# An S4-gated feed-forward kernel: two roots of the layer norm through ScalarE, one LoRA product in four row groups, and a reordered start

## The chip, the cores and the metric

The kernel runs on one core of a Trainium2 chip. The time is the device time of one launch in microseconds (us), the median of repeated runs. A profiled execution also has a span, from its first to its last recorded instruction; the rest of its time lies around the span.

The engines are named as in the profile: PE is TensorE's matmul (PEld its weight load), DVE is VectorE, ACT is ScalarE, POOL is GpSimd, SP is SyncE, which here only issues DMA transfers.

## The reference

The input `x` has 2 x 1024 tokens of 512 features, all in float32. What is computed, cut to what matters:

```python
xn = layernorm(x)                       # over the 512 features, eps 1e-5
s  = causal_convolution(xn) + D * xn    # along each row of 512, kernel from an S4 state space (64 states)
h1 = xn @ w1.T + 2 * (xn @ A1.T) @ B1.T # hidden width 1376, LoRA rank 16
h3 = xn @ w3.T + 2 * (xn @ A3.T) @ B3.T
g  = silu(h1) * h3
ffn = g @ w2.T + 2 * (g @ A2.T) @ B2.T  # back to 512
out = x + s * silu(ffn)
```

The convolution is written in the reference with FFTs over rows of 512 values.

## The kernel before, in words

The tokens are handled as four blocks of 512 (`x_in[0]` to `x_in[3]`), each of four tiles of 128 tokens by 512 features. Two blocks make a super-block. The first half of the kernel makes `g` from the blocks and stores it in DRAM (`g_dram`); the second half multiplies by `w2`, makes the convolution, the gate and the output.

The matrix products are cut in Strassen-like fashion: sums and differences of quarters of an operand are formed on DVE, and seven products (numbered 1 to 7, called steps) take the place of eight. In the first half this is done at two levels. The hidden width is split into five pairs of 256 columns (`w_pair[0]` to `w_pair[4]`) and a last part of 96 columns (`w_last`). A `Chain` is one set of seven steps. It accumulates in three PSUM banks with the tags `x`, `w` and `y` (each tag has two banks, `bank(tag)` hands them out in turn; a fourth tag is `aux`). ACT copies snapshots out of `x` and `w`, DVE adds in `y` (L779) and the kept sums (L869), ACT applies Silu (L828), POOL multiplies (L836) and adds (L869).

LoRA is folded into the weights: `lora_product` (L382) multiplies the two factors of rank 16 into a PSUM bank, and `merge` (L392) adds twice that to the weights in SBUF. The factors stand in SBUF at partitions 0, 32, 64 and 96 (the groups 0 to 3; groups 0 and 2 hold the factors of `w1`, 1 and 3 those of `w3`). `merge_pair` uses groups 0 and 1 alone and makes one half of a pair (four products); it is used for the first pair, twice. `merge_whole_pair` uses all four groups in turn (eight products), for all later pairs.

The norm: `norm_stats` (L247, L248) takes mean and variance on DVE; `norm_root` (L281 to L284) makes the reciprocal root and the shift, with eight operations of `rsqrt` (L57 to L66) on DVE; `normalize` works on ACT (tiles 0 and 2, L293) and POOL (tiles 1 and 3, L297). `norm_root` is called for block 0, for block 1, and once for blocks 2 and 3 together. Block 3's sums and squares are taken on ACT (`act_sums` L254, `act_squares` L265) with small steps on POOL. `transpose` turns the tiles on PE (L304) and copies them on ACT: into `xr` for blocks 0 and 2 (L312), into `b12` and `xr` for blocks 1 and 3 (L314, L315).

The order on each engine is the program's own (a manual schedule). In the first half it comes from a list of events with places: `at(place, what)` puts a step on a heap, which is emptied in the order of the places, and `after(delay, what)` puts one behind the current place. The places are written by hand. The steps around the change are:

- before the heap: `keep_warm` (L990, products of the identity with itself, 18 before the LoRA of the last part and 4 after it), `lora_last`, the norm of block 0 and its transposes, the statistics of block 1, `merge_last`;
- on the heap: `normalize(1)`, the last part's sums on POOL (`last_sums`), the first pair's LoRA, the transposes of block 1 into the `y` banks, the sums of token operands (`outer_token_sum`, L328) and of weights (`outer_weight_sums`, L440; `inner_weight_sum`, L452), the statistics of block 2, the sums of block 3, and so on. `inner_token_sum` (L340 to L346) makes the second level of token sums into `t_in`; the statement in `norm_root` writes `veps` (L281).

The DMA requests go out on SP (some of the first on ACT) in the order in which the program names them. Requests take turns on eight semaphores, so that a request waits until the one eight places before it has landed. The first lines of that order are:

```python
x_in = {0: load_x(0)}
...
for v, f in enumerate(factors):
    load_lora((nc.sync, nc.scalar)[v], v, *f, LSPLIT, HID)
nc.scalar.activation(warm, warm, AF.Silu)
x_in[1] = load_x(1)
w_last, s_last = load_last()
w_pair, s_pair = {0: load_pair(0)}, {c: {} for c in range(NPAIR)}
x_in[2], x_in[3] = load_x(2), load_x(3)
w_pair[1] = load_pair(1)
for v, f in enumerate(factors):
    load_lora(nc.sync, 2 + v, *f, LSPLIT, HID)
```

The activation of `warm` (L972) brings the activation table of Silu in at the start.

Of the kernel before, what the change touches and what calls it, by code (L numbers as in the profile page):

```python
# [12 lines left out]
F32 = mybir.dt.float32  # L13
# [4 lines left out]
P = 128  # L18
# [3 lines left out]
HID = 1376  # L22
# [27 lines left out]
def rsqrt(nc, pool, v, shape):  # L50


    y = pool.tile(shape, F32, tag="rs_y", name="rs_y")
    t = pool.tile(shape, F32, tag="rs_t", name="rs_t")
    part = 3.0 / 8.0
    c2 = part * 0.703952253
    nc.vector.tensor_scalar(  # L57
        y.bitcast(I32), v.bitcast(I32), -0.5, float(0x5F1FFFF9), ALU.mult, ALU.add
    )
    nc.vector.tensor_tensor(t, y, y, ALU.mult)  # L60
    nc.vector.scalar_tensor_tensor(t, t, -c2, v, ALU.mult, ALU.mult)
# [46 lines left out]
def s4_gated_ffn(  # L108
# [110 lines left out]
    def after(delay, what):  # L219
        at(now[0] + delay, what)  # L220
# [4 lines left out]
    def load_x(b):  # L225
        room = (None, None, t_in[4], t_in[6])[b]
        tiles = []
        for tt in range(NTT):
            t = value() if room is None else room[:, tt, :]
            queue = nc.scalar if b == 0 and tt % 2 else nc.sync  # L230
            queue.dma_start(out=t, in_=x[bass.ds(b * TB + tt * P, P), :])
            tiles.append(t)
        return tiles
# [41 lines left out]
            norms[b][:, :, 1], sums_of_x[b][:, 2, :], 1.0 / DIM, None, mult  # L275
        )

    def norm_root(mv, *blocks):
        n = len(blocks) * NTT
        veps = small.tile([P, n], F32, tag="veps", name="veps")  # L280
        nc.vector.tensor_scalar(veps, mv[:, :, 1], EPS, None, add)  # L281
        rstd = rsqrt(nc, small, veps, [P, n])
        shift = small.tile([P, n], F32, tag="shift", name="shift")
        nc.vector.scalar_tensor_tensor(shift, mv[:, :, 0], -1.0, rstd, mult, mult)  # L284
        for n, b in enumerate(blocks):
            norms[b] = [t[:, n * NTT : (n + 1) * NTT] for t in (rstd, shift)]
# [12 lines left out]
    def transpose(b, tiles, tag="aux"):  # L299
        sb, low = divmod(b, 2)  # L300
        for tt in tiles:
            ps = bank(tag)
            for dc in range(NDC):
                nc.tensor.transpose(  # L304
                    ps[:, dc * P : (dc + 1) * P],
                    x_in[b][tt][:, dc * P : (dc + 1) * P],
                    ident,
                )
            at_ = slice(tt * P, (tt + 1) * P)
            halves = ps.rearrange("p (c k t) -> p c k t", c=2, k=2)  # L310
            if low == 0:
                nc.scalar.copy(xr[:, 0:2, sb, :, at_], halves)  # L312
            else:
                nc.scalar.copy(b12[sb][:, :, at_], halves[:, 0])  # L314
                nc.scalar.copy(xr[:, 2, sb, :, at_], halves[:, 1])  # L315
# [64 lines left out]
    def lora_product(ps, group, dc, lo, n, start=True):  # L380
        d, h = lora_factors(group, lo, n)
        nc.tensor.matmul(  # L382
            ps,
            lhsT=d[:, dc * P : (dc + 1) * P],
            rhs=h,
            start=start,
            stop=True,
            skip_group_check=True,
        )

    def merge(to, ps):
        nc.vector.scalar_tensor_tensor(to, ps, LORA_SCALE, to, mult, add)  # L392
# [11 lines left out]
                )  # L404
        return w

    def merge_pair(c, w, half, tag="aux"):

        ps = [bank(tag), bank(tag)]
        for k in range(2):  # L410
            for v in range(2):
                n = slice(k * 2 * P, (k + 1) * 2 * P)
                lora_product(ps[v][:, n], v, 2 * half + k, PAIR_AT[c], 2 * P, k == 0)
        for v in range(2):
            to = w[:, (1, 2, 0, 3)[2 * v + half]].rearrange("p k m h -> p (k m h)")
            after(1.6 + v, lambda to=to, v=v: merge(to, ps[v]))
# [45 lines left out]
    def load_last():  # L462
        both = const.tile([P, 2, 2 * NDC * LASTR], F32, tag="w2b", name="last")
        w, s = (
            both[:, i].rearrange("p (a b h) -> p a b h", a=n, h=LASTR)
            for i, n in enumerate((2, 4))
        )
        for v, src in enumerate((w1T, w3T)):
            nc.sync.dma_start(
                out=w[:, v], in_=src[:, LAST * P :].rearrange("(dc p) h -> p dc h", p=P)  # L470
            )
        return w, s

    def lora_last():
        ps = [bank("y"), bank("y")]
# [487 lines left out]

    x_in = {0: load_x(0)}
    warm = const.tile([P, 1], F32, name="warm")
    nc.gpsimd.memset(warm, 0.0)
# [5 lines left out]
    nc.scalar.activation(warm, warm, AF.Silu)  # L972
    x_in[1] = load_x(1)
    make_upper_triangular(nc, tri, 1.0, diag=True)
    w_last, s_last = load_last()
    w_pair, s_pair = {0: load_pair(0)}, {c: {} for c in range(NPAIR)}
    x_in[2], x_in[3] = load_x(2), load_x(3)
    w_pair[1] = load_pair(1)
    for v, f in enumerate(factors):
        load_lora(nc.sync, 2 + v, *f, LSPLIT, HID)  # L980

    def other_factors():
        for v, (_, h) in enumerate(factors):
# [18 lines left out]
    ps_last = lora_last()  # L1002
    mv = norm_tile(0)
    norm_stats(0, range(NTT))
    norm_root(mv, 0)
    normalize(0)

    keep_warm(primed[1], 4)
    transpose(0, range(NTT))
    mv = norm_tile(1)  # L1010
    norm_stats(1, range(2))
    merge_last(w_last, ps_last, 0)
    norm_stats(1, range(2, NTT))
    norm_root(mv, 1)
    merge_last(w_last, ps_last, 1)
    mv_late = norm_tile(2, 3)
    ab_last = last_operands(w_last, s_last)

# [573 lines left out]
```

## Time and profile before

| what | value |
|---|---|
| time, median of 3 runs | 442.49 us (442.27 to 443.13) |
| profiled execution: time / span | 442.57 us / 440.8 us |
| PE busy | 433.5 us, 98% of the span |
| DVE busy | 316.9 us, 72% |
| POOL busy | 209.3 us, 47% |
| ACT busy | 144.2 us, 33% |
| granted PE clock | 0.998 of full speed |
| DMA moved | 53.61 MB, mean 122 GB/s over the span |
| chain that ended last | PE 84%, DVE 10%, issue 2%, ACT 2%, DMA 1% |

The page gives shares over the whole span. The start can be read only from the timelines: they list each engine's instructions in order of time, with start, length, engine, line, operation, output, input, and in brackets the idle time before it and what ended that. A count such as x8 may name records: an ordinary float32 product leaves two records, a transpose one. The chain of waits follows the last instruction back, at each step to what released it or to the instruction before it on its engine.

In the first 20 us the transfers run at 218 to 379 GB/s and the DMA engines are full from 5 us on; PE has its first product at 1.37 us (the priming ones) and its first transposes at 10.45.

### The profile page before, as it was taken

The numbers are of one execution on the slowest core, as the hardware profiler recorded it, in microseconds if no ns is written. First come the engines' busy times: TensorE is split into PE (matmuls) and PEld (weight loads), VectorE is DVE, ScalarE is ACT, GpSimd is POOL, SyncE is SP. The second block draws the span as 40 slices with busy tenths as digits, with TensorE's granted clock in tenths as the row PEclk, the third lists the DMA queues.
The fourth block names the chain that finished last, engine by engine and source line by source line (L and its number), as shares of the span: only waits on it lengthen the run. The fifth ranks groups of instructions, "written<-read, shape, count | busy, mean of one in ns | idle before, by whom it ended". The sixth has DMA issues, their size and how long they took to land.

```text
span 440.8 us, 5156 instructions
## 1 busy us (share of the span) xinstructions
PE 433.5 (98%) x1704; PEld 268.5 (61%) x1704; DVE 316.9 (72%) x534; ACT 144.2 (33%) x296; POOL 209.3 (47%) x156
## 2 busy tenths in 40 slices
PE   7999999999999999999999999999999999999996
PEld 7545333444444444444443447888898999999995
DVE  5899999946974597469746796979786875753234
ACT  2777242453245324532453242211101212112221
POOL 2325469995689368936894469400000123222221
PEclk9999999999999999999999999999999999999999
DMA  8921304025002400350045526395902833423211
GB/s 258 370 66 47 116 0 149 24 72 168 25 24 96 143 24 25 99 160 24 25 148 187 167 90 214 112 348 200 342 22 75 306 115 95 144 97 95 88 57 48
DMA packets 35466, 53.61 MB, mean 122 GB/s; under 512 B 4688, under 2 KB 21520, under 8 KB 35312
## 3 DMA queue, kind: packets, MB, share of 16 engines
q1 hardware_dynamic: 35088, 52.69, 36.9%
q10 hardware_dynamic: 352, 0.60, 0.4%
q8 instruction: 13, 0.21, 0.2%
q14 instruction: 13, 0.11, 0.1%
HBM read 33.88 MB, written 19.40 MB: 121 GB/s over the span
## 4 chain that ended last, share of the span: by engine, by line
PE 84%; DVE 10%; issue 2%; ACT 2%; DMA 1%; POOL 0%; SPq 0%; DVEq 0%; POOLq 0%
PE x L755 42%; PE y L755 21%; PE w L755 11%; PE aux L929 4%; PE w L929 2%; DVE s L452 1%; DVE t_in L342 1%; DVE xt L328 1%; DMA s<-in_x_dram 1%; DVE t_in L340 1%; DVE w L440 1%; DVE s L779 1%; PE y L382 1%; PE y L528 1%; PE aux L710 1%
## 5 line engine op out<-in xcount | busy, mean ns | idle before, releaser
L1310 POOL TENSOR_TENSOR o<-o,xin 128x512 f32<-128x512 f32 (+1 forms) x17 | 23.3, 1369 | 132.9 <-DVE o L1309 132.9
L836 POOL TENSOR_TENSOR s<-c,s 128x512 f32<-128x512 f32 (+1 forms) x44 | 63.1, 1439 | 16.1 <-ACT c L828 10.9
L775 ACT COPY s<-x 128x512 f32<-128x512 f32 (+1 forms) x54 | 31.6, 584 | 86.8 <-PE x L755 86.7
L755 PE MATMUL x<-t_in,s 128*128 128x512 f32 (+1 forms) x148 | 55.4, 501 | 0.0
L779 DVE TENSOR_TENSOR s<-s,y 128x512 f32<-128x512 f32 (+1 forms) x54 | 36.0, 679 | 17.2 <-PE y L755 12.1
L869 POOL TENSOR_TENSOR s<-ua_three,s 128x512 f32<-128x512 f32 x20 | 35.9, 1793 | 25.7 <-DVE s L779 25.7
L755 PEld LDWEIGHTS x<-t_in,s 128*128 128x128 f32 x148 | 26.6, 190 | 23.3 <-issue 12.0
L869 POOL TENSOR_TENSOR ua_three<-ua_three,s 128x512 f32<-128x512 f32 x20 | 33.0, 1652 | 15.1 <-DVE s L779 15.1
L755 PE MATMUL y<-t_in,s 128*128 128x256 f32 (+1 forms) x108 | 35.8, 458 | 0.0
L1332 ACT COPY z<-x 128x256 f32<-128x256 f32 x24 | 8.8, 371 | 70.5 <-PE x L755 70.4
L1307 DVE TENSOR_TENSOR aux<-aux,m 128x384 f32<-128x384 f32 x32 | 18.1, 565 | 15.8 <-PE aux L929 14.3
L869 POOL TENSOR_TENSOR s<-u_three,s 128x512 f32<-128x512 f32 x20 | 28.5, 1430 | 1.8 <-ACT c L828 1.0
L828 ACT ACTIVATE c<-c 128x512 f32<-128x512 f32 x40 | 25.2, 632 | 10.0 <-DVE c L869 10.0
L755 PEld LDWEIGHTS y<-t_in,s 128*128 128x128 f32 x108 | 20.2, 190 | 11.1 <-issue 9.3
L793 ACT COPY w<-x 128x512 f32<-128x512 f32 (+1 forms) x37 | 21.1, 570 | 12.2 <-PE x L755 12.2
L869 POOL TENSOR_TENSOR u_three<-ua_three,u_three 128x512 f32<-128x512 f32 x10 | 15.6, 1557 | 11.6 <-DVE u_three L779 11.5
L755 PE MATMUL x<-t_in,w 128*128 128x512 f32 x40 | 20.9, 603 | 0.0
L755 PE MATMUL x<-xr,s 128*128 128x512 f32 x40 | 20.6, 616 | 0.2 <-DVE ua_one L869 0.2
L755 PE MATMUL x<-xt,w 128*128 128x512 f32 x40 | 20.7, 598 | 0.0
L755 PE MATMUL x<-xr,w 128*128 128x512 f32 x40 | 20.6, 614 | 0.0
L755 PE MATMUL x<-xt,s 128*128 128x512 f32 x40 | 20.4, 592 | 0.0
L440 DVE TENSOR_TENSOR w<-w 128x512 f32<-128x512 f32 x20 | 20.1, 1015 | 0.1
(302 smaller groups left out, 906.0 us busy)
## 6 DMA issues: line engine op xcount, KB each, us to landing
g_dram<-s SPq DMA_DIRECT2D x40, 256.0 KB, 2.1
g<-g_dram SPq DMA_DIRECT2D x10, 512.0 KB, 5.6
xin<-in_x_dram SPq DMA_DIRECT2D x16, 256.0 KB, 2.8
out_dram<-o SPq DMA_DIRECT2D x14, 256.0 KB, 2.0
t_in<-g_dram SPq DMA_DIRECT2D x6, 512.0 KB, 4.2
w<-in_w1T_dram SPq DMA_DIRECT2D x10, 256.0 KB, 3.3
w<-in_w3T_dram SPq DMA_DIRECT2D x10, 256.0 KB, 5.0
t_in<-in_x_dram SPq DMA_DIRECT2D x8, 256.0 KB, 5.5
```

Source lines behind the costliest of these rows:

```text
L440: nc.vector.tensor_tensor(*sums[name])
L755: nc.tensor.matmul(ps[:, cols], lhsT=lhsT, rhs=rhs if parts == 1 else rhs[:, cols], start=first and i == 0 and part == 0, stop=i == len(pa ...
L775: nc.scalar.copy(t, self.x)
L779: nc.vector.tensor_tensor(t, t, self.y, add)
L793: nc.scalar.copy(self.w, self.x)
L828: nc.scalar.activation(c, c if src is None else src, AF.Silu)
L836: nc.gpsimd.tensor_tensor(g, act, g, mult)
L869: (nc.vector if o < 20 else nc.gpsimd).tensor_tensor(to, a, b, add)
L929: nc.tensor.matmul(to[:, n * P : (n + 1) * P], lhsT=x_, rhs=by, start=start, stop=True, skip_group_check=True,)
L1307: nc.vector.tensor_tensor(y[:, P:], y[:, P:], m[:, n * P : (n + 3) * P], add)
L1310: (nc.vector if last else nc.gpsimd).tensor_tensor(o, o, self.xin[h][:, cols], add)
L1332: nc.scalar.copy(t, xb)
```

## The change

The change has four parts, and moves some places with them.

- `norm_root` gets a flag `on_act`, set for blocks 0 and 1. Then `refined` takes the root on ACT (`AF.Sqrt`, with `eps` as its bias), the reciprocal on DVE, and one Newton step on DVE (three operations). `norm_root` of blocks 2 and 3 keeps `rsqrt`. The first activation of `warm` is now a Sqrt, and a second one, of Silu, follows the root of block 1. There is one priming product more (5).
- The first pair's LoRA is made by `merge_whole_pair` in one lot, into the two `y` banks and the two `aux` banks, ahead of block 1's transposes. `merge_pair` goes. The first tile of block 1 is transposed into a borrowed `x` bank, the other three into the `y` banks.
- The factors of groups 2 and 3, needed for that, are requested before the first pair's weights rather than after the second pair's.
- The request for `w1` of the last part stands ahead of block 1's tiles; that for `w3` stays behind them.
- Places: three of block 2's four statistics move behind the first pair's sums (0.84 to 0.9, before -5.2 to -3.6); the merge of the last part's `w3` comes ahead of the second root; `normalize(2)` and `normalize(3)` move from 7.3 and 7.7 to 7.7 and 7.75. With that ACT copies block 1's four tiles before the last part's first Silu, and a snapshot of `ua_three` before it normalizes block 2.

```diff
+    def refined(mv, veps):
+        shape = list(veps.shape)
+        y = small.tile(shape, F32, tag="rs_y", name="rs_y")
+        t = small.tile(shape, F32, tag="rs_t", name="rs_t")
+        root = small.tile(shape, F32, tag="root", name="root", bufs=1)
+        nc.scalar.activation(root, mv[:, :, 1], AF.Sqrt, bias=eps)
+        nc.vector.tensor_scalar(veps, mv[:, :, 1], EPS, None, add)
+        nc.vector.reciprocal(y, root)
+        nc.vector.tensor_tensor(t, y, y, mult)
+        nc.vector.scalar_tensor_tensor(t, t, -0.5, veps, mult, mult)
+        nc.vector.scalar_tensor_tensor(y, t, 1.5, y, add, mult)
+        return y
...
-        rstd = rsqrt(nc, small, veps, [P, n])
+        if on_act:
+            rstd = refined(mv, veps)
+        else:
+            nc.vector.tensor_scalar(veps, mv[:, :, 1], EPS, None, add)
+            rstd = rsqrt(nc, small, veps, [P, n])
...
-    nc.scalar.activation(warm, warm, AF.Silu)
+    nc.scalar.activation(warm, warm, AF.Sqrt)
+    w_last, s_last, load_of_last = load_last()
+    load_of_last(0)
     x_in[1] = load_x(1)
+    load_of_last(1)
     make_upper_triangular(nc, tri, 1.0, diag=True)
-    w_last, s_last = load_last()
+    for v, f in enumerate(factors):
+        load_lora(nc.sync, 2 + v, *f, LSPLIT, HID)
     w_pair, s_pair = {0: load_pair(0)}, {c: {} for c in range(NPAIR)}
     x_in[2], x_in[3] = load_x(2), load_x(3)
     w_pair[1] = load_pair(1)
-    for v, f in enumerate(factors):
-        load_lora(nc.sync, 2 + v, *f, LSPLIT, HID)
...
-    norm_root(mv, 0)
+    norm_root(mv, 0, on_act=True)
     normalize(0)
-    keep_warm(primed[1], 4)
+    keep_warm(primed[1], 5)
...
     norm_stats(1, range(2, NTT))
-    norm_root(mv, 1)
     merge_last(w_last, ps_last, 1)
+    norm_root(mv, 1, on_act=True)
+    nc.scalar.activation(warm, warm, AF.Silu)
...
-    at(-9, lambda: merge_pair(0, w_pair[0], 0))
-    at(-3.8, lambda: merge_pair(0, w_pair[0], 1))
-    for i in range(2):
-        at(-6 + i, lambda i=i: transpose(1, range(2 * i, 2 * i + 2), "y"))
+    at(-9, lambda: merge_whole_pair(
+        0, w_pair[0], [bank("y"), bank("y")], (1.6, 1.7, 1.8, 1.9)))
+    at(-6, lambda: transpose(1, (0,), "x", True))
+    at(-5.9, lambda: transpose(1, range(1, NTT), "y"))
...
-        at(-6 + 0.8 * tt, lambda tt=tt: norm_stats(2, (tt,)))
+        at((-6, 0.84, 0.85, 0.9)[tt], lambda tt=tt: norm_stats(2, (tt,)))
...
-    at(7.3, lambda: normalize(2))
-    at(7.7, lambda: normalize(3, (0,)))
+    at(7.7, lambda: normalize(2))
+    at(7.75, lambda: normalize(3, (0,)))
```

More of the change, by code (lines that the diff above doesn't have):

```diff
@@ L276, in act_variances, with norm_root @@
         )
-    def norm_root(mv, *blocks):
+    def refined(mv, veps):
[10 more added lines that the diff above has]
+        return y
+    def norm_root(mv, *blocks, on_act=False):
         n = len(blocks) * NTT
         veps = small.tile([P, n], F32, tag="veps", name="veps")
-        nc.vector.tensor_scalar(veps, mv[:, :, 1], EPS, None, add)
-        rstd = rsqrt(nc, small, veps, [P, n])
+        if on_act:
[3 more added lines that the diff above has]
+            rstd = rsqrt(nc, small, veps, [P, n])
         shift = small.tile([P, n], F32, tag="shift", name="shift")
@@ L297, in normalize, with transpose @@
                 nc.gpsimd.tensor_scalar(t, t, rstd[:, one], shift[:, one], mult, add)
-    def transpose(b, tiles, tag="aux"):
+    def transpose(b, tiles, tag="aux", borrow=False):
         sb, low = divmod(b, 2)
         for tt in tiles:
-            ps = bank(tag)
+            ps = bank(tag, borrow)
             for dc in range(NDC):
@@ L405, in load_pair @@
         return w
[L407 to L416, printed above, removed]
     def merge_whole_pair(c, w, first=None, delays=(1.15, 2.3, 4.3, 4.4)):
@@ L467, in load_last, with load @@
         )
-        for v, src in enumerate((w1T, w3T)):
+        def load(v):
             nc.sync.dma_start(
-                out=w[:, v], in_=src[:, LAST * P :].rearrange("(dc p) h -> p dc h", p=P)
+                out=w[:, v],
+                in_=(w1T, w3T)[v][:, LAST * P :].rearrange("(dc p) h -> p dc h", p=P),
             )
-        return w, s
+        return w, s, load
     def lora_last():
@@ L965, in s4_gated_ffn @@
     warm = const.tile([P, 1], F32, name="warm")
-    nc.gpsimd.memset(warm, 0.0)
+    eps = const.tile([P, 1], F32, name="eps")
+    for t, v in ((warm, 0.0), (eps, EPS)):
+        nc.gpsimd.memset(t, v)
     make_identity(nc, ident)
@@ L1058, in s4_gated_ffn @@
     at(-9.9, lambda: last_sums(w_last, s_last))
-    at(-9, lambda: merge_pair(0, w_pair[0], 0))
-    at(-3.8, lambda: merge_pair(0, w_pair[0], 1))
-    for i in range(2):
-        at(-6 + i, lambda i=i: transpose(1, range(2 * i, 2 * i + 2), "y"))
+    at(
+        -9,
+        lambda: merge_whole_pair(
+            0, w_pair[0], [bank("y"), bank("y")], (1.6, 1.7, 1.8, 1.9)
+        ),
+    )
+    at(-6, lambda: transpose(1, (0,), "x", True))
+    at(-5.9, lambda: transpose(1, range(1, NTT), "y"))
     for n, name in enumerate((3, 2, 1)):
```

## The prediction

> **What bounds the kernel now.** I read the page first, then the chain of waits, then the timeline of each engine up to 75 us, where all the edits lie or take effect. TensorE (PE) is busy 98% of the span, so the question for a change at the start is whether work taken off PE there stays off. The chain that ended last, in order of time:
>
> ```profile
> 9.58 0.82 ACT s L293
> 12.99 1.78 PE x L755 x8
> ...
> 31.63 1.52 ACT t_in L293 x2
> 34.34 1.20 DVE w L392 x2
> 35.54 2.12 DVE s L452
> ...
> 52.23 2.64 DVE t_in L342
> 55.47 2.20 DVE t_in L340
> 58.86 2.20 DVE t_in L342
> ...
> 65.41 1.28 DVE xt L346
> 66.69 0.84 issue
> 69.35 1.12 PE x L755 x2
> ```
>
> Three stages are to be seen. Until about 21 us the norms and PE alternate. From 31 to 69 us the chain is VectorE (DVE). After 73.95 us it is PE to the end. In the VectorE timeline, one operation follows the other from 29.61 to beyond 74 us, with one idle of 0.23 us:
>
> ```profile
> 20.99 1.29 DVE L328 TENSOR_TENSOR xt<-xr,b 128x512 f32<-128x512 f32 x2 [0.64 <-ACT xr L315]
> 29.61 0.17 DVE L281 TENSOR_SCALAR veps<-mv 128x8 f32<-128x8 f32 x1
> 33.65 0.69 DVE L779 TENSOR_TENSOR ua_three<-ua_three,y 128x512 f32<-128x512 f32 x1 [0.23 <-ACT ua_three L775]
> 58.79 2.28 DVE L342 TENSOR_TENSOR t_in<-t_in,xt 128x2048 f32<-128x2048 f32 x1
> ```
>
> PE takes its data from that stretch. Its product at 55.52 needs the sum that starts at 52.23 and a bank that DVE frees at 55.4, the one at 61.12 needs the sum that ends at 61.07, and the one at 69.35 is recorded as waiting for DVE. So a microsecond won on PE before 31 us becomes a wait at 55.52, unless DVE too arrives earlier. I therefore follow DVE's clock: its arrival at the total of 33.65.
>
> The other rows that carry the sum, from the timelines of PE, ScalarE (ACT) and GpSimd (POOL):
>
> ```profile
> 10.45 1.09 PE L304 MATMUL aux<-ident,s 128*128 128x128 f32 x8 [0.85 <-ACT s L293]
> 14.70 1.13 PE L382 MATMUL aux<-lo_h,lo_d 16*128 16x256 f32 x8
> 15.76 1.96 PE L755 MATMUL w<-xr,last 128*96 128x512 f32 x4
> 30.99 1.13 PE L755 MATMUL x<-xt,w 128*128 128x512 f32 x2
> 2.59 1.28 ACT L972 ACT_TABLE_LOAD   x1 [2.59 <-issue]
> 20.52 0.44 ACT L315 COPY xr<-y 128x256 f32<-128x256 f32 x1
> 35.43 1.26 POOL L836 TENSOR_TENSOR s<-c,s 96x512 f32<-96x512 f32 x1
> ```
>
> **The first root.** Eight DVE operations of `rsqrt` (7.80 to 9.34) go; a reciprocal and three others come, at the old spacing of 0.195 us (a reciprocal of 128x4 has a row, 0.18 us). The reciprocal waits for ACT's Sqrt, which runs beside `veps` from 7.60. A Sqrt of 128x4 has no row. The nearest is the 128x1 activation of L972 with 0.20 us, and a bias read from memory costs about 0.10 (0.718 with one in L265, 0.622 without in L254); so 0.20 to 0.30, and I take 0.30. With 0.03 for the handover, `shift` starts at 7.93 + 4 x 0.195 = 8.71 in place of 9.38. The first normalized tile follows 0.67 us earlier, at 9.77. The fifth priming product ends at 8.43 + 5 x 0.27 = 9.78, so PE begins transposing there: 0.67 earlier. The extra product is covered by the normalization; without that cover it would cost 0.27.
>
> **LoRA four at a time.** Before, eight products use two row groups, in two lots of 1.06 us (14.70 to 15.76 and 20.91 to 21.97). The other pair's eight in four groups take 29.92 to 30.99, 1.07 us. PE sheds 1.05 us. Now block 0 is followed by: LoRA 14.03 to 15.10, then the product into `w`, the transposes, and no LoRA after them.
>
> **The requests.** `w1` of the last part (192 KB) moves ahead of block 1's four tiles, which landed at 7.6, 8.3, 9.0 and 9.7. The 192 KB had taken 0.7 us of the stream (9.7 to 10.4), so they land at most that much later, 8.3 to 10.4. Their statistics now start at 8.8, 9.6, 10.9 and 11.7: hidden. The four small LoRA requests pass twelve large ones and the second pair's four on SP. For the first pair's weights (12.3 to 14.6) that means between 0.4 us (140 KB at about 380 GB/s) and 1.8 (four issues of 0.45) more, so 14.6 becomes 15.0 to 16.4; the merge that needs the last of them would start at 15.8, and a bank must be free at 18.0, so even the upper end is hidden. Block 3 then lands at 20.4 to 21.8 in place of 20.0; its sums start at about 20.9, so they end up to 0.9 late, and the variances at about 28.2 to 29.1, still before DVE asks.
>
> **The second root and the table.** ACT's four copies of block 0 end at 13.61 - 0.67 = 12.94; the Sqrt after them ends at 13.24, the load of Silu's table (1.28) at 14.52, `warm` (0.20) at 14.72. Queued behind them are the copy into `w` (0.56) and two normalizations. PE's product into `w` waits for that copy: 15.30, though LoRA was done at 15.10. Before it was 15.76. So of 1.72 won (0.67 + 1.05), 0.46 is left here by the table load and the order; the second LoRA lot comes off later.
>
> The only load in the trace ran on an idle engine, and `warm` followed 0.01 us later. The Trainium skill ("ScalarE: Activation LUTs", section "What ACT_TABLE_LOAD costs") gives each switch a drain of about 1.38 us on top of 1283 ns. By that page the sum below would be some 1.4 us higher; no row here shows a load behind other activations.
>
> By rows, what comes on top of the load lies between nothing and one more load (1.28); I take nothing, the row, and keep the upper end for a rival.
>
> **Transposes and the sums behind them.** They start at 15.30 + 1.79 = 17.09. ACT's first copy comes 0.64 later, 17.73; the four copies of tiles 0 and 1 (0.27 apart) end at 18.94, which frees the bank for tile 3; its own copies start at 19.62 and end at 20.30, in place of 20.96. DVE's token sums start at 20.33 (before 20.99). The merges run 15.1 to 17.5 and one statistic to 18.4, all before that.
>
> Now the order on DVE counts. Before, 14 operations of 0.60 us led from 20.99 to 29.4, and `veps` started at 29.61 (POOL's variances came at 29.58). Now there are 12 (two merges gone ahead), but three statistics with their aggregates (0.82 each) stand behind them: 20.33 + 7.2 + 2.47 = 30.00. From `veps` to the total of 33.65 there are ten small operations (1.93), two merges and a total (1.8): 3.73, and 0.31 of waiting for ACT's copy of `ua_three`. That copy is now queued ahead of the normalizations and its product is early, so the wait goes. The total starts at 30.00 + 3.73 = 33.73: 0.08 us later than before. DVE had time for these statistics while it waits for ACT (18.4 to 20.3), and does not use it.
>
> PE meanwhile is ahead: its product on the token sums starts at 20.33 + 0.65 = 21.0 rather than 21.97. That lead of 1.0 us dies at 55.52.
>
> One contact with POOL changes. At 35.43 POOL's product began 0.02 us before L452, which took 2.19 in place of 1.09. Now POOL comes 0.39 later (its normalizations follow `veps`) and DVE 0.08, so DVE goes first and the next L452 waits about 1.1 instead: about -0.1 us by the end of both. Every later operation on DVE keeps its order.
>
> **The sum.** The profiled execution took 442.57 us, 440.8 of it span and 1.8 around it; it is 0.08 above the median of the three runs. Its 442.57 + 0.08 - 0.1 is 442.55, and against the median 442.5. That is no change: 0.2% (0.9 us) is about what a measurement of this kernel can tell from none. This case's own range is 442.0 to 443.1.
>
> **Rivals.**
> 1. *PE's lead is kept.* If the late sums could go unwaited, or DVE's stretch had slack that the timeline hides, the end moves by 1.0 to 1.2: 441.4. For it speaks PE's 98%; against it the products at 55.52 and 61.12, which read what DVE has just written. Chance 0.14.
> 2. *POOL's turns fall otherwise.* Between 35 and 74 us DVE's operations are stretched by some 5 us beside POOL's (L452 by 1.10, two L440 by 1.07, L342 by 0.90, two L346 by 0.97, L344 by 1.10, each against 0.58 to 0.60 for 512 elements). One turn of 1.1 less gives 441.4, one more 443.6. For it speaks the 0.02 us at 35.43; against it that POOL's later products mostly wait for DVE's own totals, and shift with them. Chance 0.11 less, 0.07 more.
> 3. *Slower: the table load lasts longer behind a running Sqrt.* The copy into `w` ends at 15.27, already after LoRA's 15.10, so each tenth more is a tenth more at the end of the copies, at `veps` and at the finish. It decides from a price of about 2.2 us for the load (0.9 above its row). With one more load-length, 442.5 + 1.28 = 443.8. For it speaks that the load now stands behind other work; against it the 0.01 us after the one seen. With late landings at the same place: 0.21.
>
> **Numbers.** The forecast holds 0.47; faster is 0.14 + 0.11 = 0.25, slower 0.07 + 0.21 = 0.28. The range reaches to the first two rivals and to most of the third: 441.3 to 443.7.
>
> **What would show it.** In the changed profile: transposes from 9.8; eight LoRA products in about 1.07 us from 14.0; the copy into `w` at about 14.7, after one load of 1.28; token sums at 20.3; `veps` at 30.0; the total of `ua_three` at 33.7 without idle; PE waiting near 55.5 for DVE. `veps` well before 29.5, or PE passing 69 us more than 0.5 us early, would make me wrong, and so would a gap behind the table load.

## The result, and the profile after

The kernel after takes 443.29 us (median of 20 runs, 442.30 to 445.61) beside 442.38 us before (20 runs, 441.79 to 443.88): a ratio of 1.0019, 95% interval 1.0011 to 1.0027. It is slower by about 0.9 us (0.5 to 1.2 by the interval): little, but clear of the noise. The forecast was 442.5 us, "no change". The stated range of 441.3 to 443.7 holds the result, the narrower 442.0 to 443.1 that the prediction gave its own case does not, and the number is 0.8 us too low. Six of the 20 runs lie above 443.7.

The profiled execution of after took 443.36 us, 441.5 of it span (before 442.57 and 440.8). The program has moved in its file: the matmul is L764 (before L755), the DVE totals L788 (L779), the token sums L345 (L328) and L357 to L363 (L340 to L346), the weight sums L446 and L458 (L440 and L452), `veps` of blocks 2 and 3 L298 (L281), a merge L409 (L392), LoRA's products L399 (L382), transposes L321 (L304) and `normalize` L310 and L314 (L293 and L297).

The chain that ended last in after; the columns are start, length (both us), engine, tile and line:

```profile
1.40 7.21 PE w L1003 x36
9.67 1.31 PE w L1003 x10
13.31 1.78 PE x L764 x8
21.25 2.50 DVE xt L345 x4
34.95 0.60 DVE ua_three L788
53.40 2.63 DVE t_in L359
```

The first piece is new in this list: until 11 us the chain now runs through PE's warm-up, where before it ran through ACT's normalization at 9.58. From 21 us on it is DVE. In before the stretch from 21.5 to 29.6 ran through ACT's sums of block 3 and POOL's variances, which came at 29.58, just ahead of `veps` at 29.61. The same stretch in DVE's timeline; the bracket gives the idle time before an operation and what ended it:

```profile
21.25 1.29 DVE L345 TENSOR_TENSOR xt<-xr,b 128x512 f32<-128x512 f32 x2 [1.77 <-ACT xr L332]
31.08 0.17 DVE L298 TENSOR_SCALAR veps<-mv 128x8 f32<-128x8 f32 x1
34.87 0.68 DVE L788 TENSOR_TENSOR ua_three<-ua_three,y 128x512 f32<-128x512 f32 x1
59.95 2.28 DVE L359 TENSOR_TENSOR t_in<-t_in,xt 128x2048 f32<-128x2048 f32 x1
```

DVE now sits idle for 1.77 us ahead of the token sums (before 0.64), starts them 0.26 us later, and reaches the total of `ua_three`, the place whose time the prediction followed, 1.22 us later (34.87, before 33.65). From there to 59.95 the distance is what it was (25.08 and 25.14). PE and ACT ahead of that:

```profile
10.82 1.04 PE L321 MATMUL aux<-ident,s 128*128 128x128 f32 x8
16.18 1.96 PE L764 MATMUL w<-xr,last 128*96 128x512 f32 x4
56.68 1.13 PE L764 MATMUL x<-t_in,s 128*128 128x512 f32 x2 [0.37 <-DVE c L878]
13.83 0.30 ACT L284 ACTIVATE root<-mv,eps 128x4 f32<-128x4 f32 x1
14.14 1.28 ACT L1029 ACT_TABLE_LOAD   x1
15.44 0.20 ACT L1029 ACTIVATE warm<-warm 128x1 f32<-128x1 f32 x1
15.55 0.58 ACT L802 COPY w<-x 96x512 f32<-96x512 f32 x1
20.84 0.38 ACT L332 COPY xr<-y 128x256 f32<-128x256 f32 x1
```

The transposes start at 10.82 where 9.78 was forecast, and everything up to the last copy of block 1 is late by about as much.

PE is 1.15 us later at 75.10 (before 73.95) and 1.40 later at its product of 424.32 (422.92). DVE's last operation is also 1.40 later (ends at 438.91 and 437.51), but the span is only 0.7 longer: the last two output requests of 64 KB landed in 1.6 us (median) where before's took 2.4. That is no chance of one execution: these requests took 1.6 us in all eleven profiles of kernels built on after, and 2.0 to 2.4 in the three of kernels built on before. Which edit brings it stays open.

### The profile page after: what moved, and what is told of

The parts are those of the page before. It is cut to its first block, busy times and chain, and to the rows that moved or that the text cites. A ratio compares the mean times of both kernels' runs of the same rounds, so it can differ in the third digit from the quotient of the medians.

```text
span 441.5 us, 5160 instructions
## 1 busy us (share of the span) xinstructions
PE 434.2 (98%) x1706; PEld 269.5 (61%) x1706; DVE 314.7 (71%) x526; ACT 146.1 (33%) x300; POOL 211.2 (48%) x157
## 4 chain that ended last, share of the span: by engine, by line
PE 85%; DVE 12%; issue 1%; ACT 0%; POOL 0%; DVEq 0%; POOLq 0%
PE x L764 41%; PE y L764 21%; PE w L764 11%; PE aux L938 4%; PE w L938 2%; DVE xt L345 2%; PE w L1003 2%; DVE w L446 1%; PE y L399 1%; DVE s L458 1%; DVE t_in L359 1%; DVE s L788 1%; DVE t_in L357 1%; PE y L537 1%; PE aux L719 1%
## 5 line engine op out<-in xcount | busy, mean ns | idle before, releaser
L764 PE MATMUL x<-t_in,s 128*128 128x512 f32 (+1 forms) x148 | 55.4, 501 | 0.4 <-DVE c L878 0.4
L788 DVE TENSOR_TENSOR s<-s,y 128x512 f32<-128x512 f32 (+1 forms) x54 | 36.0, 679 | 17.6 <-PE y L764 12.1
L764 PEld LDWEIGHTS x<-t_in,s 128*128 128x128 f32 x148 | 26.6, 190 | 23.7 <-issue 12.0
L764 PE MATMUL y<-t_in,s 128*128 128x256 f32 (+1 forms) x108 | 35.8, 458 | 0.0
L764 PEld LDWEIGHTS y<-t_in,s 128*128 128x128 f32 x108 | 20.2, 190 | 11.1 <-issue 8.6
L764 PE MATMUL x<-t_in,w 128*128 128x512 f32 x40 | 20.9, 603 | 0.0
L764 PE MATMUL x<-xr,s 128*128 128x512 f32 x40 | 20.6, 616 | 0.1
L764 PE MATMUL x<-xr,w 128*128 128x512 f32 x40 | 20.6, 614 | 0.0
L764 PE MATMUL x<-xt,w 128*128 128x512 f32 x40 | 20.6, 597 | 0.0
L764 PE MATMUL x<-xt,s 128*128 128x512 f32 x40 | 20.4, 592 | 0.0
L764 PE MATMUL y<-xt,s 128*128 128x512 f32 x40 | 19.9, 595 | 0.0
```

The source lines that it names most:

```text
L764: nc.tensor.matmul(ps[:, cols], lhsT=lhsT, rhs=rhs if parts == 1 else rhs[:, cols], start=first and i == 0 and part == 0, stop=i == len(pa ...
L788: nc.vector.tensor_tensor(t, t, self.y, add)
```

## The experiments

Theory A is the prediction's: DVE's arrival at `ua_three` sets the finish, and what counts is DVE's work between the token sums and that total. Its rivals: PE's own time counts, or the table load costs what is lost. All medians below are of repeated runs beside runs of the kernel before on the same chip: 442.6 us for the first four kernels, 442.87 for the next four, 442.78 for the last four.

### First: the statistics and the root

The four statistics of block 2 cost DVE 0.8 us each with their aggregates. After puts three of them behind the token sums. Three kernels move them, a fourth takes the Sqrt away. Further on, "all early" is `e1_stats_back`, "three early" `e2_three_early` (it moves two of after's three late statistics back), "roots on DVE" `e3_rsqrt`.

`e1_stats_back`: after, all four at the places of before.

```diff
-        at((-6, 0.84, 0.85, 0.9)[tt], lambda tt=tt: norm_stats(2, (tt,)))
+        at(-6 + 0.8 * tt, lambda tt=tt: norm_stats(2, (tt,)))
```

> The changed kernel with one edit undone: block 2's four statistics stand at their old places, ahead of the token sums. Theory A (DVE's arrival at the total of ua_three sets the end): in the profile of the changed kernel the merges ended at 18.58, so four statistics of 0.80 end at 21.8 and the token sums start there instead of at 21.25; the root of blocks 2 and 3 then follows after twelve operations of 0.60, at 29.1 in place of 31.08, and the total starts near 32.9 in place of 34.87. The time falls by 1.3 to 1.9 us against the changed kernel, to 441.4 to 442.0. Rival (PE's place at the first product on the token sums sets the end): that product comes 0.5 us later, 22.6 in place of 22.1, and the time rises by 0.5 to 443.8.

`e2_three_early`: after, three of them early.

```diff
-        at((-6, 0.84, 0.85, 0.9)[tt], lambda tt=tt: norm_stats(2, (tt,)))
+        at((-6, -5.8, -5.7, 0.9)[tt], lambda tt=tt: norm_stats(2, (tt,)))
```

> The changed kernel with two of the three late statistics put back ahead of the token sums (three early, one late). Theory A: DVE waits from 19.4 to 21.25 in the changed kernel, and 1.64 us of statistics fit there, so the token sums keep their start; the root comes at 21.25 + 7.2 + 0.8 = 29.3 in place of 31.08. The time falls by 1.2 to 1.8 us against the changed kernel, to 441.5 to 442.1, below the kernel before. Rival (PE's place sets the end): PE's order up to 31 us is as in the changed kernel, so the time stays at 443.3.

`e3_rsqrt`: after, both roots by `rsqrt` on DVE, Silu's table at the start, four warm-up products instead of five.

```diff
-    nc.scalar.activation(warm, warm, AF.Sqrt)
+    nc.scalar.activation(warm, warm, AF.Silu)
-    norm_root(mv, 0, on_act=True)
+    norm_root(mv, 0)
-    keep_warm(primed[1], 5)
+    keep_warm(primed[1], 4)
-    norm_root(mv, 1, on_act=True)
-    nc.scalar.activation(warm, warm, AF.Silu)
+    norm_root(mv, 1)
```

> The changed kernel with the roots of blocks 0 and 1 made by rsqrt on DVE again, Silu's table loaded at the start, and four priming products; all else as changed. Theory A: the first normalized tile comes 0.5 us later, but PE's priming ended at 10.8 in the changed kernel's profile, so between 0.1 and 0.7 us of that reaches the token sums and the end: 443.4 to 444.0. Rival (the table load behind the Sqrt holds ACT's copy into w and is what was lost): the load goes, the copy starts when its product is done, and the time falls by 0.3 to 1.3 us, to 442.0 to 443.0.

`e4_before_late`: before, with three statistics at after's places.

```diff
-        at(-6 + 0.8 * tt, lambda tt=tt: norm_stats(2, (tt,)))
+        at((-6, 0.84, 0.85, 0.9)[tt], lambda tt=tt: norm_stats(2, (tt,)))
```

> The kernel before with one edit of the change alone: three of block 2's statistics stand behind the first pair's sums. Theory A: the token sums start at 20.99 as before; the root of blocks 2 and 3 comes three statistics later, at 31.9 in place of 29.61, and the total of ua_three at 35.5 in place of 33.65. The time rises by 1.6 to 2.3 us, to 444.0 to 444.7. Rival (PE's place sets the end): PE's order is unchanged up to 31 us and the time stays at 442.4.

Measured, in this order: 444.95 (443.28 to 446.21; ratio 1.0052, 1.0032 to 1.0072), 444.90 (440.93 to 447.14; 1.0043, 1.0016 to 1.0069), 444.71 (443.30 to 446.04; 1.0047, 1.0032 to 1.0062) and 445.16 us (444.73 to 446.17; 1.0059, 1.0046 to 1.0072).

The last fits A: the places alone cost before 2.6 us, where 1.6 to 2.3 were expected. In its profile `veps` comes at 31.76 (forecast 31.9) and the total at 35.80 (35.5). The rest has a second cause, which PE's timeline there shows:

```profile
35.82 2.06 PE L755 MATMUL x<-xr,w 128*128 128x512 f32 x2 [2.24 <-ACT ua_three L775]
```

PE stood idle for 2.24 us behind the late DVE, and then the granted clock read 0.50 for 3.41 us (35.87 to 39.28); the same product took 1.12 us in before. The one run of the five with a mean granted clock of 1.0 took 444.73 us, 2.1 above before; the other four, at 0.994 to 0.996, took 444.95 to 446.17. Half a clock for 3.41 of 442 us lowers the mean by 0.004.

The first two missed: early statistics should have gained, and lost. But three of the twelve runs of three early took 440.93 to 441.9, as forecast or a little less, and the others 443.65 to 447.14. The profiled execution is one of the long ones, 447.14 us. POOL's timeline there, then ACT's and DVE's:

```profile
24.87 3.88 POOL L260 TENSOR_SCALAR act_sums<-act_sums 128x4 f32<-128x4 f32 x1 [5.69 <-ACT c L254]
28.72 0.22 POOL L261 TENSOR_SCALAR mv<-act_sums 128x4 f32<-128x4 f32 x1
32.28 0.22 POOL L274 TENSOR_SCALAR mv<-act_sums 128x4 f32<-128x4 f32 x1 [3.34 <-ACT c L265]
```

```profile
28.78 0.72 ACT L265 ACTIVATE c<-t_in,act_sums 128x512 f32<-128x512 f32 x1 [3.19 <-POOL act_sums L260]
```

```profile
27.98 0.69 DVE L446 TENSOR_TENSOR w<-w 128x512 f32<-128x512 f32 x1
32.54 0.17 DVE L298 TENSOR_SCALAR veps<-mv 128x8 f32<-128x8 f32 x1 [3.05 <-POOL mv L274]
```

The step at 24.87 scales 128x4 numbers. In the profile of after it took 0.28 us (0.22 in before):

```profile
24.76 0.28 POOL L260 TENSOR_SCALAR act_sums<-act_sums 128x4 f32<-128x4 f32 x1 [5.68 <-ACT c L254]
```

Here it lasts 3.88, in `e1_stats_back` 4.80 and in `e3_rsqrt` 3.34. It falls among DVE's sums of two operands, which follow one another without a gap, and in all three profiles it ends 0.08 us after the last of them (28.75 and 28.67 here, 30.04 and 29.96 in `e1_stats_back`, 28.63 and 28.55 in `e3_rsqrt`). ACT's squares of block 3 wait for it, POOL's variances wait for those, and `veps` waits for the variances. That is a new theory, B: this step is held while DVE's sums follow each other, in some executions and not in others. The Trainium skill ("SBUF — State Buffer", section "SBUF: two separate sides") states that a DVE operation with two SBUF inputs and a GpSimd operation that reads SBUF exclude each other for a whole instruction. These profiles agree, and show more: the step is passed over by several sums in a row. In the profile of `e2_three_early` a half clock comes on top: PE waited 2.52 us for ACT, the granted clock read 0.50 from 31.91 to 38.73, and DVE then waited 1.17 and 0.77 us more for PE and ACT. `e3_rsqrt` is inconclusive for that reason: what the Sqrt alone brings can't be read from it.

### Second: the same without POOL's small steps

All four kernels take block 3's two means and its variances from POOL to ACT:

```diff
-        nc.gpsimd.tensor_scalar(sums[:, 1, :], sums[:, 0, :], -1.0 / DIM, None, mult)
-        nc.gpsimd.tensor_scalar(norms[b][:, :, 0], sums[:, 0, :], 1.0 / DIM, None, mult)
+        nc.scalar.activation(sums[:, 1, :], sums[:, 0, :], AF.Copy, scale=-1.0 / DIM)
+        nc.scalar.activation(norms[b][:, :, 0], sums[:, 0, :], AF.Copy, scale=1.0 / DIM)
...
-        nc.gpsimd.tensor_scalar(
-            norms[b][:, :, 1], sums_of_x[b][:, 2, :], 1.0 / DIM, None, mult
-        )
+        nc.scalar.activation(
+            norms[b][:, :, 1], sums_of_x[b][:, 2, :], AF.Copy, scale=1.0 / DIM
+        )
```

`e5_early_no_pool` does it to three early, `e6_after_no_pool` to after, `e7_all_early_no_pool` to all four early, `e8_before_no_pool` to before.

> The kernel after with three of block 2's four statistics at early places, as in the run with three early, and block 3's two means and its variances scaled on ACT in place of POOL. Theory (POOL's 128x4 step, 0.22 to 0.28 us where it gets in, is held 3.3 to 4.8 us between VectorE's sums, and that alone made the runs with early statistics late): veps near 29.2 to 29.9, total of ua_three near 32.9 to 33.6, median 441.2 (440.8 to 441.9) with all runs within about 1.5 us, as the fastest runs of three early (440.9 to 441.9). Rival (the spread comes from elsewhere: priming, transfers, the order on VectorE itself): median 444 to 445 and a spread of several us, as three early had.

> The kernel after with block 3's two means and its variances scaled on ACT in place of POOL, nothing else. Theory: the profile of after already had POOL's step in at 0.28 us, so the order on VectorE stays: veps near 31.1, total of ua_three near 34.9, median 443.0 (442.5 to 443.4), and the runs of 444 to 445.6 that after showed are gone. Rival (POOL has no part in after's time): median 443.3 with the same spread of 3 us. Second rival (after's lateness is itself POOL's): under 442.3.

> The kernel after with all four of block 2's statistics at the places of the kernel before, and block 3's two means and its variances scaled on ACT in place of POOL. Theory: as with three early without POOL, less one statistic of 0.6 us from VectorE's row after 22 us, but part of it lands in front of the merges: total of ua_three 32.6 to 33.6, median 441.2 (440.6 to 441.9). Rival (early statistics delay the merges and with them the clock): 443 to 445, as with POOL (444.95).

> Control: the kernel before with block 3's two means and its variances scaled on ACT in place of POOL. Theory (POOL's step got in at 0.22 to 0.28 us in the profile of before): no change of the usual run, median 442.3 (442.0 to 442.6), the few runs above 443 gone. Rival (POOL's step costs before something in every run): under 441.9. Second rival (ACT's own row is what counts): over 442.9.

| kernel | median us | spread | ratio to before, interval |
|---|---|---|---|
| three early, no POOL step | 442.26 | 441.52 to 445.20 | 0.9987, 0.9972 to 1.0001 |
| after, no POOL step | 443.41 | 442.85 to 443.86 | 1.0011, 1.0001 to 1.0020 |
| all early, no POOL step | 442.33 | 441.82 to 444.77 | 0.9993, 0.9977 to 1.0008 |
| before, no POOL step | 442.60 | 442.07 to 443.89 | 0.9995, 0.9985 to 1.0006 |

Early statistics, which lost 2.3 us with POOL's step, now come out a little under before, in medians 0.6 and 0.5 us, though each interval still reaches 1. So B holds for them: with three tiny operations moved, eleven of the twelve runs of three early lie within 441.5 to 442.7. After keeps its median and loses its runs above 443.9. Three statistics early instead of one is worth 442.26 to 443.41, that is 1.15 us, and all four instead of one 442.33 to 443.41, 1.08 us; in the profiles of three early and after `veps` comes at 29.29 and 31.09.

The forecasts of 441.2 were too low by 1.1. In the profile of three early without POOL's step 0.51 us of that stands as an idle of DVE behind `veps`, which no profile with the steps on POOL has; it may be a price of this edit. And one run in twelve of three early, and some of all early, are still at 443 to 445. The profile of all early is one (444.37 us). Its DVE waits, summed by cause (total, times, longest), show what else varies:

```profile
DVE veps L298 <- ACT mv L274: 2.2, 1, 2.2
DVE w L409 <- DMA w<-in_w3T_dram: 0.9, 1, 0.9
DVE stats L247 <- DMA s<-in_x_dram: 0.5, 1, 0.5
```

Block 1 and the first pair's `w3` land late there. The token sums slip to 22.32, PE's product behind them too, and ACT's copy of that product (27.64, after 2.52 us of waiting) stands ahead of the squares. PE's timeline there shows why the copy is so late:

```profile
23.12 3.61 PE L764 MATMUL y<-xt,last 128*96 128x512 f32 x4 [2.39 <-DVE xt L345]
```

In after this product took 1.93 us. Again the granted clock read 0.50 for 3.41 us, from 23.23 to 26.64, behind the idle of 2.39. The mean granted clock of each run says that this is the rule for the long ones: of the 83 runs without POOL's steps (those with the old requests left out) six took more than 444 us, five of them at a mean of 0.994 to 0.996; no run below 444 us has less than 0.997. The half clock is not certain: PE idled as long, 2.51 us, in `e1_stats_back` and `e3_rsqrt` without it. So what is left of the spread is late landings and late DVE work, which leave PE idle, and the half clock that such an idle sometimes brings.

### Third: the warm-up, the requests and the table load

`e9_short_priming`: after without POOL's steps, with less warm-up. The term that missed is the end of the warm-up; here it is cut.

```diff
-        keep_warm(ps, 9, True)
+        keep_warm(ps, 8, True)
-    keep_warm(primed[1], 5)
+    keep_warm(primed[1], 2)
```

> The kernel after with block 3's means and variances on ACT, and a shorter warm-up of TensorE: two times eight products ahead of the first LoRA in place of two times nine, and two behind it in place of five. Theory (the prediction's one mis-sized term is the end of the warm-up, 10.8 in place of 9.78; the rest of its sum holds): transposes near 9.9, copy into w near 14.8, token sums on VectorE near 20.4, total of ua_three near 34.1 to 34.5, and the median 0.7 to 0.9 us under the kernel after without POOL's steps (443.41 beside a before of 442.87), so level with before to within 0.2%. Rival (another chain ends nearly as late: root of block 1, 1.28 us of table load, copy into w; or the transfers of block 1): w product still near 16.0 to 16.2 with an idle of 0.5 or more ahead of it that ends with ACT's copy, token sums at 21.0 to 21.3, median less than 0.3 us lower.

`e10_old_requests`: after without POOL's steps, with the requests in the order of before.

```diff
-    load_of_last(0)
     x_in[1] = load_x(1)
+    load_of_last(0)
     load_of_last(1)
     make_upper_triangular(nc, tri, 1.0, diag=True)
-    for v, f in enumerate(factors):
-        load_lora(nc.sync, 2 + v, *f, LSPLIT, HID)
...
     w_pair[1] = load_pair(1)
+    for v, f in enumerate(factors):
+        load_lora(nc.sync, 2 + v, *f, LSPLIT, HID)
```

> The kernel after with block 3's means and variances on ACT, and the requests in the order of the kernel before: block 1, then both halves of the last chunk, the first pair, blocks 2 and 3, the second pair, and the remaining LoRA factors last. Theory (the new order of requests costs nothing that counts, since VectorE has 1.0 to 1.8 us idle before the token sums): median within 0.3 us of the kernel after without POOL's steps. Rival (last w1 ahead of block 1 and LoRA factors ahead of the first pair make block 1's statistics and the merges wait, 0.36 and 0.64 us in that kernel's profile): those two waits are gone, token sums 0.3 to 0.7 us earlier, median 0.3 to 0.7 us lower. Second rival (the first pair's LoRA now needs its factors early): merges wait for LoRA's factors, later by 1 us or more, slower.

`e11_early_short`: three early without POOL's steps, and the warm-up of `e9_short_priming`.

> Candidate: three statistics early, block 3's means and variances on ACT, and the shorter warm-up of TensorE. Theory (the warm-up's end sets the row): token sums near 20.7 (VectorE's three statistics end there), total of ua_three near 33.0, median 0.3 to 0.6 us under three early without POOL's steps (442.26 beside a before of 442.87), so 0.2% to 0.3% under before. Rival (table load behind the root of block 1): as three early without POOL's steps to within 0.15 us.

`e12_early_short_table`: the same, with the second root on DVE and the table load behind the first Sqrt.

```diff
     norm_root(mv, 0, on_act=True)
+    nc.scalar.activation(warm, warm, AF.Silu)
-    norm_root(mv, 1, on_act=True)
-    nc.scalar.activation(warm, warm, AF.Silu)
+    norm_root(mv, 1)
```

> Candidate: as the one with early statistics and shorter warm-up, with the second root on VectorE (the bit trick of the kernel before, 1.8 us there) and Silu's table loaded right behind the first Sqrt in place of behind the second. Theory (the table load of 1.28 us ahead of the copy into w is the next bound): normalize of block 0 some 0.4 us later (9.6 to 9.8), transposes near 10.2 to 10.4, no idle of TensorE ahead of the w product, w product near 15.4 to 15.7, token sums near 20.7, median 0 to 0.4 us under the candidate without this step. Rival (the load in front of normalize of block 0 delays everything behind it by as much): 0.3 to 0.5 us over it.

| kernel | median us | spread | ratio to before, interval |
|---|---|---|---|
| after, short warm-up | 443.44 | 442.37 to 443.94 | 1.0010, 1.0002 to 1.0019 |
| after, old requests | 456.22 | 455.73 to 456.44 | 1.0298, 1.0284 to 1.0311 |
| early, short warm-up | 441.93 | 441.23 to 444.06 | 0.9982, 0.9971 to 0.9992 |
| the same, table load moved | 442.31 | 441.31 to 444.75 | 0.9993, 0.9979 to 1.0006 |

The shorter warm-up did not move after (443.44, 443.41 without it). Its profile, PE:

```profile
10.34 1.09 PE L321 MATMUL aux<-ident,s 128*128 128x128 f32 x8 [0.77 <-ACT s L310]
15.75 1.96 PE L764 MATMUL w<-xr,last 128*96 128x512 f32 x4
```

The median is what the rival said; the rows lie between the two (product into `w` at 15.75 without idle, token sums at 20.82, total of `ua_three` at 34.86, with the same 0.51 us behind `veps` in it as in `e6_after_no_pool`, whose total came at 35.30). PE was ready and waited 0.77 us for ACT's normalized tile, since block 0 had landed late (DVE's third statistic starts at 6.34 after a wait of 0.70 for the transfer; 6.03 in after). So behind the warm-up stands another end, about as late. A third is the table load: in the profiles of `e1_stats_back`, `e2_three_early` and `e6_after_no_pool` the product into `w` waits 0.5 to 0.6 us for ACT's copy behind that load. In `early, short warm-up` (its profile is of a run of 444.06 us) the transposes start at 9.92, and still

```profile
16.37 1.96 PE L764 MATMUL w<-xr,last 128*96 128x512 f32 x4 [0.44 <-ACT w L802]
18.49 0.69 DVE L409 SCALAR_TENSOR_TENSOR w<-y,w 128x512 f32<-128x512 f32 x1 [2.03 <-DMA w<-in_w3T_dram]
```

(PE's and DVE's timelines.) Block 1 landed late there, so the second Sqrt stood at 14.03, and the load and the copy behind it ended at 16.32. In the kernel with the table load moved, that idle is gone (product at 15.41) and the median is no better: in its profile DVE starts the token sums at 21.34 straight behind a statistic, so DVE's own row, with a wait of 0.37 for `w3` in it, had become the last.

The old requests lost 12.8 us. DVE's timeline there:

```profile
25.71 1.29 DVE L409 SCALAR_TENSOR_TENSOR w<-y,w 128x512 f32<-128x512 f32 x2 [11.11 <-PE y L399]
```

LoRA four at a time needs the factors that before asks for last; PE waited 8.91 us for their landing, and the granted clock read 0.50 from 16.71 to 30.36, so that the product into `w` took 3.73 us (1.96 in after). The order of the requests is part of the LoRA edit. What the 192 KB of `w1` alone do was not tried by itself.

The kernel with early statistics, no small steps on POOL and the short warm-up beats before: 441.93, ratio 0.9982 (0.9971 to 0.9992).

### What all profiles say together

Each row is one profiled execution: DVE's start of the first total of `ua_three`, the whole time, and the difference.

| kernel | arrival us | time us | difference |
|---|---|---|---|
| three early, no POOL step | 33.49 | 441.67 | 408.18 |
| early, short warm-up, table moved | 33.54 | 442.43 | 408.89 |
| before | 33.65 | 442.57 | 408.92 |
| before, no POOL step | 34.01 | 442.67 | 408.66 |
| after, short warm-up | 34.86 | 443.44 | 408.58 |
| after | 34.87 | 443.36 | 408.49 |
| early, short warm-up | 35.12 | 444.06 | 408.94 |
| after, no POOL step | 35.30 | 443.77 | 408.47 |
| before, late statistics | 35.80 | 446.17 | 410.37 |
| all early, no POOL step | 35.84 | 444.37 | 408.53 |
| after, roots on DVE | 36.16 | 444.46 | 408.30 |
| all early | 37.55 | 445.80 | 408.25 |
| three early | 38.34 | 447.14 | 408.80 |
| after, old requests | 47.47 | 456.18 | 408.71 |

Over 14 us of arrival the difference stays within 408.2 to 408.9, with one exception, the kernel before with late statistics. There PE stands idle for 0.85 us at 240.82, which no row of before has, for a merge of DVE into `w_a` (L392) that itself waited 3.46 us for its weights to land (2.09 in before). After a half clock PE can also be the later of the two: in that profile and in that of three early the chain runs through PE's products from 60 us on.

## Why the prediction was right, and where it was off

**Right: which engine's clock counts.** The table shows it, and PE's product at 56.68 waits for DVE, as the prediction said of 55.5. Rival 1 (PE's lead is kept) is out.

**Right: the order on DVE.** From the token sums to `veps` it gave 9.67 us; 9.83 were measured (21.25 to 31.08). From there to the total: 3.73 and 3.79, without the idle of before, as said. To the next level of sums at 53.40: 18.53 us (18.58 before), a gain of 0.05 where 0.1 was named; rival 2 (POOL's turns fall otherwise) did not occur between 35 and 74 us.

**Right: the sizes of the new operations.** The Sqrt took 0.30, the load 1.28; `warm` began 0.02 us after it, and the copy came at once. The eight LoRA products took from 15.02 to 16.18, 1.16 (1.07 forecast). Rival 3's longer load is out. The Trainium skill ("ScalarE: Activation LUTs", section "What ACT_TABLE_LOAD costs") adds a drain of about 1.38 us; in this trace there is none behind the Sqrt, and the measurement decides.

**Off by 0.92: the start of the token sums**, 20.33 forecast and 21.25 measured. That and 0.16 and 0.06 from the two stretches on DVE make the 1.14 between the forecast arrival (33.73) and the measured one. The step that failed is "The fifth priming product ends at 8.43 + 5 x 0.27 = 9.78, so PE begins transposing there". The transposes began at 10.82. ACT's normalized tile was ready by about 10.0 (9.16 and 0.82 us for one tile), 0.2 later than forecast, mostly since block 0 landed later; the other 0.8 is the warm-up, and the fifth product, taken as covered by the normalization, was not. The 36 records of the first warm-up took 7.21 us, 6.07 before, though the code is the same. By windows, these records alone; the columns are the window, its length, PE's busy time and count, PEld's, the granted clock, and two of DMA. Before, and then after:

```profile
4.40:5.40 1.00, 1.00 (x8) 1.00 (x8) 1.00 1.21 356
5.40:6.40 1.00, 1.00 (x12) 1.00 (x11) 1.00 0.91 120
```

```profile
5.40:6.40 1.00, 1.00 (x6) 1.00 (x6) 1.00 1.12 128
6.40:7.40 1.00, 1.00 (x7) 1.00 (x6) 1.00 1.13 293
7.40:8.40 1.00, 1.00 (x10) 1.00 (x9) 1.00 1.05 332
```

PE first works off some 6 or 7 in a microsecond and then 10 to 12; by windows of 0.2 us the step lies near 5.2 us in before and near 7.6 in after. The granted clock column reads 1.00 throughout, but the clock record in the trace has its first entry, of full clock, at just these moments, 5.15 and 7.56; the column shows 1.00 where there is no entry. Over the eleven profiles with nine and nine products the first entry lies between 4.60 and 7.56 us, and these records took 5.80 to 7.21 us in the same order; the three profiles of the kernel before, with and without an edit, have 6.07 to 6.62. So the moment belongs to the execution, not to the kernel. The Trainium skill ("TensorE: Matmul & The Clock Gate", section "Part 1: The HAM clock gate (the "warmup" mystery)") describes such a step, set by a free-running window.

I took one execution's moment for a constant. But the short warm-up shows that the warm-up alone is not the answer: the landing of block 0, the warm-up, and the second Sqrt with the load behind it end within some 0.6 us of each other, and the latest of them decides. A gain worked out along one of several nearly equal ends is an upper bound; the prediction carried 0.46 us of gain to the product into `w` and the whole 0.66 to the token sums. In the six profiles with after's roots, requests and full warm-up the product into `w` starts between 15.51 and 16.65, in the mean at 16.13; 15.30 was forecast. The three of before have 15.51 to 16.25, in the mean 15.84. Nothing of the 0.46 forecast is to be seen there. That the number is off by only 0.8 us is in part luck: in this execution the total came 1.14 us late, and the quicker landing of the last outputs, which the prediction did not have, gave about 0.7 back.

**Right that time, and not in general: POOL's variances "still before DVE asks".** In the profile of after they came in time. With the same POOL steps, the profiles of all early, three early and roots on DVE show `veps` waiting 3.87, 3.05 and 1.47 us for them. The prediction took these steps as cheap because their rows were.

**Hidden as said, in that execution:** the merges did not wait for `w3`. In seven of the later profiles they did, 0.4 to 2.0 us. Late landings were put under rival 3; that part of it was real.

So the loss of 0.9 us is the three statistics behind the token sums (1.08 us between after and all early, both without POOL's steps), less the little that the other edits gain together (all early without POOL's steps stands 0.27 under before without them, less than either spread). What the Sqrt, the LoRA in one lot and the request for `w1` bring each was not separated.

## What to carry to other kernels

Find the engine whose arrival sets the end, and follow that single moment: here it gave the time of nearly every variant to 0.4 us. When a step is moved into that engine's busy stretch, its whole length counts, while idle time just ahead of the stretch is free. Where three chains end within half a microsecond or so, shortening one of them gains nearly nothing, and one profile does not tell which will be last in the next execution.

## What was not expected of the hardware

- A POOL operation of 0.22 us on 128x4 numbers can last 3.3 to 4.8 us when DVE's two-operand sums follow one another without a gap. It is hit or miss: the same kernel took 440.93 and 447.14 us. On ACT the step took 0.21 us.
- PE's step from slow to fast during the warm-up came at 7.56 us in one execution and at 4.60 in another. The column of the granted clock reads 1.00 ahead of it too; only the clock record, which begins at that moment, and the spacing of the products show it.
- After PE had stood idle for 2.2 to 2.5 us the granted clock fell to 0.50 in three profiles, for 3.41, 3.41 and 6.83 us, and in two others with an idle of 2.51 us it did not. A late DVE then costs more than its own delay.
- In the profiles of five kernels without POOL's steps DVE stands still for 0.51 us between `veps` and the operation after it, which waits for nothing else that is shown; in the other nine profiles, those with POOL's steps among them, it follows within 0.1 us. That stays open.
